# Token blocks 1 to 3 transposed by VectorE in 32 by 32 blocks by way of DRAM, and a first layer norm by pairs of tiles with the constants loaded behind x

## The chip, the core and the metric

The kernel runs on one core of a Trainium2 chip. The time is the device time of one execution in microseconds (us). The core has five engines that run side by side, each in the order of its own instruction queue: TensorE (PE in the profile; PEld is its weight load), VectorE (DVE), ScalarE (ACT), GpSimd (POOL) and SyncE (SP). DMAs are issued from the queues of SP, ACT and POOL and carried out by 16 DMA engines.

## The reference

The input x is 8 sequences of 256 tokens with 512 features, float32. One layer is computed:

```python
xn = _layernorm(x)                       # over the 512 features
s = attention(xn, wq, wk, wv, wo)        # 32 heads of 128, 8 key/value heads, RoPE,
                                         # causal mask, rescaled scores, softmax
g = silu(ffn(xn, router_w, A, B))        # 4 experts of rank 16, the best 2 per token
out = x + s * g
```

## The kernel before

**Tiling.** The 2048 tokens are worked on in four token blocks (`NTB`) of 512 tokens, two sequences each; a block has four tiles of 128 tokens (`NT`). Within a block there are eight steps, one for each key/value head `g`. A step computes, for the next step, a *quad* of projections (`quad`, L486: the queries of four heads, and now and then keys or values) and, for earlier steps, the scores and the softmax (`softmax`), the weighted values (`values`) and a part of the output projection (`out_project`). Projections are multiplied by a scheme of Strassen's kind with seven products (`piece`, L518), each of 8 weight loads and 8 matmuls in the trace. Their names in the trace are pa, pd and pe with k, q or v behind (keys, queries, values); po belongs to the output projection, sc to the scores, av to the weighted values.

**The input of a block.** The projections need the normalised x transposed, features on partitions. It lies in one tile, XB (`acts[tb][0]`), as four quarters; XT (`acts[tb][1]`) holds four sums and differences of the quarters, made by VectorE (`add_up`, L362). There is one buffer for XB and one for XT, so XB of the next block can only be written when the last projection of the block has read it (the hold `x_hold`, room `X=1`).

`norm(tb)` (L309) makes them. For each of four tiles it loads x on SP (`load`, L319), takes mean and variance on VectorE (`statistics`), the root on ScalarE (`root`), the reciprocal (`invert`) and the normalised tile xn (`normalise`) on VectorE. Then TensorE transposes it against an identity matrix into PSUM (`turn`, L349: four transposes of 128x128, called xp in the trace), and ScalarE copies it to XB (`read`, L354). For block 0 the root is taken tile by tile, for the other blocks once for four tiles.

**The start.** Block 0 has nothing to hide behind. SP loads four tiles of x, then the first weights w (`blocks_of`, L408). ScalarE's queue loads three constants at once: the table tab (L1284: cosines, sines, masks), ra (L1285: router and expert weights, rows of 272 B) and bt (L1286). After the key projection the expert scores of the block are computed (`route`, L1137, called lme in the trace: 16 matmuls on XB and ra).

**The softmax's way through DRAM.** `softmax` normalises the probabilities p on VectorE, turns them there in 32 by 32 blocks (`transpose`, L744, tile blocks), writes them to DRAM with four DMAs on SP (`spread`, L755, tile there) and reads them back transposed with one DMA (`gather`, L764, tile pT), which av needs.

**What sets the order.** No engine's order is written out by hand. Each piece of work is a job with an engine, an estimated duration, a lag after its end (for a DMA) and the jobs it comes after (`Plan.add`, L181). TensorE's pieces are laid in a row (`lay`, L191), which gives each a due time; the others' due times follow from it backwards (L196 to L201). `Plan.run` (L195) then plays the whole in time and emits, for each engine, the ready job that is due first and has room in its buffers (`opens`, `closes`). The engines' queues keep this order on the chip. `norm` of the next block is added in step g = 6, and its four transposes are laid among that step's later pieces (L1323 to L1326):

```python
if tb + 1 < NTB and g == KV - 2:
    turns = norm(tb + 1)
    for t in range(NT):
        later[t] = later[t] + [turns[t]]
```

Of the kernel before, what the change touches and what calls it, by code (L numbers as in the profile page):

```python
# [37 lines left out]
F32 = mybir.dt.float32  # L38
# [6 lines left out]
P = 128  # L45
# [211 lines left out]
def layer(ctx: ExitStack, tc: tile.TileContext, x, wquad, woquad, raT, bT, table, out):  # L257
# [12 lines left out]
    ps_sc = pool("ps_sc", 2, space=PSUM)  # L270
    ps_av = pool("ps_av", 2, space=PSUM)
    bounce = pool("bounce", 4, space=DRAM)
    store = pool("store", 1, space=DRAM)

    tab = keep.tile([P, C_END], F32, tag="tab", name="tab")
# [18 lines left out]
    def hold(tag):  # L294
        return Hold(rooms[tag])
# [6 lines left out]

    keys, vals, queries, probs, attn, acc = {}, {}, {}, {}, {}, {}
    begun = []
    gates, sums_of, acts, weights, x_hold = {}, {}, {}, {}, {}

    def norm(tb):  # L309


        n = f"{tb}"
        xs, box = {}, {}
        xh = [hold("x") for _ in range(NB)]
        mh = [hold("m") for _ in range(NT)]
        ph = [hold("mm") for _ in range(NT)]
        x_hold[tb] = hold("X")

        def load(t):  # L319
            if t % 2 == 0:  # L320
                xs["x", t // 2] = x_pool.tile([P, 2, D], F32, tag="x", name=f"x{tb}_{t}")
            xs[t] = xs["x", t // 2][:, t % 2, :]
            nc.sync.dma_start(out=xs[t], in_=x[bass.ds(tb * TB + t * P, P), :])

        def statistics(t):
            if t == 0:
                box["mv"] = one.tile([P, NT, 2], F32, tag="mv", name=f"mv{n}")
                box["r"] = one.tile([P, NT], F32, tag="rstd", name=f"rstd{n}")
            st = two.tile([P, 6], F32, tag="st", name=f"st{tb}_{t}")
            nc.vector.bn_stats(out=st, in_=xs[t])  # L330
            nc.vector.bn_aggr(out=box["mv"][:, t, :], in_=st)

        def variance(ts):
            nc.vector.tensor_scalar_add(box["r"][:, ts], box["mv"][:, ts, 1], EPS)

        def root(ts):
            nc.scalar.sqrt(box["r"][:, ts], box["r"][:, ts])

        def invert(ts):
            nc.vector.reciprocal(box["r"][:, ts], box["r"][:, ts])  # L340

        def normalise(t):
            xn = box[t] = two.tile([P, D], F32, tag="m", name=f"xn{tb}_{t}")
            nc.vector.tensor_scalar(
                out=xn, in0=xs[t], scalar1=box["mv"][:, t, 0:1], scalar2=box["r"][:, t : t + 1],
                op0=ALU.subtract, op1=ALU.mult,
            )

        def turn(t):  # L349
            pt = box["p", t] = ps_mm.tile([P, 2, 2, P], F32, tag="mm", name=f"xp{tb}_{t}")  # L350
            for c in range(DC):
                nc.tensor.transpose(pt[:, c // 2, c % 2, :], box[t][:, bass.ts(c, P)], ident)

        def read(t):  # L354
            if t == 0:
                acts[tb] = (
                    one.tile([P, 2, NB, 2, S], F32, tag="XB", name=f"XB{tb}"),
                    one.tile([P, 4, 2, S], F32, tag="XT", name=f"XT{tb}"),
                )
            nc.scalar.copy(acts[tb][0][:, :, t // 2, :, bass.ts(t % 2, P)], box["p", t])  # L360

        def add_up(i):  # L362
            XB, XT = acts[tb]
            b11, b12, b21, b22 = XB[:, 0, 0], XB[:, 0, 1], XB[:, 1, 0], XB[:, 1, 1]
            t1, t2, t3, t4 = (XT[:, k] for k in range(4))

            a, b = ((b12, b11), (b22, t1), (b22, b12), (b21, t2))[i]
            nc.vector.tensor_sub(XT[:, i], a, b)

        issues = []  # L370
        for t in range(NT):
            issues.append(
                add("sp", 0.3, lambda t=t: load(t), after=issues[-1:],
                    opens=[xh[t // 2]] if t % 2 == 0 else [])
            )
        loads = [
            add("dma", 0.0, lambda: None, after=[issues[t]], lag=8.5 if tb else 5.0 + 1.3 * t)
            for t in range(NT)
        ]
        sts = [add("dve", 0.9, lambda t=t: statistics(t), after=[loads[t]]) for t in range(NT)]  # L380
        begun.extend(issues)
        done = []

        for ts in [slice(0, NT)] if tb else [slice(t, t + 1) for t in range(NT)]:
            v = add("dve", 0.1, lambda ts=ts: variance(ts), after=sts[ts])
            r = add("act", 2.8 if tb else 0.2, lambda ts=ts: root(ts), after=[v])
            done += [add("dve", 0.1, lambda ts=ts: invert(ts), after=[r])] * len(sts[ts])
        reads, pieces = [], []
        for t in range(NT):
            xn = add("dve", 0.4, lambda t=t: normalise(t), after=[done[t]], opens=[mh[t]], closes=[xh[t // 2]])  # L390
            tp = add("pe", 0.5, lambda t=t: turn(t), after=[xn, identity], opens=[ph[t]], closes=[mh[t]])
            opens = [x_hold[tb]] if t == 0 else []
            after = [tp] + reads[:1]
            reads.append(
                add("act", 0.5, lambda t=t: read(t), after=after, opens=opens, closes=[ph[t]],
                    near=(tp, 0.5))
            )
            pieces.append(tp)
        t1 = add("dve", 0.61, lambda: add_up(0), after=reads)
        t2 = add("dve", 0.61, lambda: add_up(1), after=[t1])  # L400
        t3 = add("dve", 0.61, lambda: add_up(2), after=reads)
        t4 = add("dve", 0.61, lambda: add_up(3), after=[t2])
        acts[tb, "B"], acts[tb, "T"] = reads, [t1, t2, t3, t4]
        return pieces

    def blocks_of(tb, room, ring, source, kept, key, form, first):  # L408
# [1 line left out]

        n = f"{room}{tb}_{key}"
        box, there, holds = {}, {}, {}
        order = (A11, A21, A22, A12, S1, S2, S4) if not tb else form.order

        def load(i):
            w = box[i] = ring.tile([P, 2, 2 * P], F32, tag=room, name=f"{n}_{i}")
# [24 lines left out]
        for i in order[:4]:  # L441
            there[i] = add(
                "sp" if first else "pool", 0.4 if first else 0.8, lambda i=i: load(i), after=issue,
                opens=[holds[i]], lag=10.0 if first else 6.0,
            )
        for i, (to, a, b, op) in enumerate(form.steps):
            there[to] = add(
# [38 lines left out]
    def quad(tb, which, out, room, rows, name):  # L486
# [15 lines left out]
        def product(bank, i, half, b, t, first):  # L502
            if first:
                box[bank] = new(bank)
            ps = box[bank]
            xb = acts[tb][0][:, half, b] if t is None else acts[tb][1][:, t]

            for m in range(2):
                for c in range(2):
# [8 lines left out]
        def piece(bank, i, half, b, t, first, after):  # L518
            return add(
                "pe", 1.73, lambda: product(bank, i, half, b, t, first),  # L520
                after=[there[i]] + (XB if t is None else [XT[t]]) + after,
                opens=[{"pa": pa, "pd": pd, "pe": pe}[bank]] if first else [],
                closes=[wh[i], x_hold[tb]],
            )
# [44 lines left out]
    def rope(src, of, dst, opens, after, name):  # L569
# [21 lines left out]
        def turn():  # L591
# [3 lines left out]
        s1 = add("act", 1.0, lambda: swap(1), after=[s0], closes=[of])  # L595
        c = add(
            "dve", 1.14, lambda: nc.vector.tensor_mul(dst(), split(src()), wide(C_COS)),
            after=after + [tables], opens=opens, closes=[of],
        )
        t = add("dve", 1.14, turn, after=[s1])  # L600
        return add(
# [529 lines left out]
    def experts(tb):  # L1131
# [2 lines left out]
        n = f"e{tb}"  # L1134
        box = {}

        def route():  # L1137
            XB = acts[tb][0]
            lm = box["lm"] = ps_av.tile([P, NT, E + E * R], F32, tag="av", name=f"lm{n}")
            for t in range(NT):  # L1140
                for c in range(DC):
                    nc.tensor.matmul(
                        lm[:, t, :],
                        lhsT=XB[:, c // 2, t // 2, c % 2, bass.ts(t % 2, P)],
                        rhs=ra[:, c, :],
                        start=(c == 0),
                        stop=(c == DC - 1),
                    )

        def rank_them():  # L1150
            lm = box["lm"]
# [43 lines left out]
            nc.scalar.copy(box["gmT"], box["gp"])  # L1195

        lh, th = hold("av"), hold("av")
        p1 = add("pe", 3.75, route, after=acts[tb, "B"] + [tables], opens=[lh], closes=[x_hold[tb]])
        r1 = add("dve", 2.0, rank_them, after=[p1], near=(p1, 2.0))
        r2 = add(  # L1200
            "act", 0.3, lambda: nc.scalar.activation(box["gate"], box["gate"], AF.Exp),
            after=[r1], near=(p1, 4.0),
# [35 lines left out]
            return p  # L1238

        gates[tb] = []  # L1240
        return [p1], [p2], [[silu(t)] for t in range(NT)]

# [20 lines left out]
    def lay(pieces):  # L1265
        for piece in pieces:
            plan.lay(piece)
# [12 lines left out]
    def clear():  # L1280
        nc.gpsimd.memset(probs_sb, 0.0)

    def load_tables():
        nc.scalar.dma_start(out=tab, in_=table)  # L1284
        nc.scalar.dma_start(out=ra, in_=raT.rearrange("(c p) m -> p c m", p=P))  # L1285
        nc.scalar.dma_start(out=bt, in_=bT)  # L1286

    identity = add("pool", 1.5, lambda: make_identity(tc.nc, ident), near=None)
    tables = add("act", 2.0, load_tables, lag=4.0)
    cleared = add("pool", 2.0, clear)  # L1290

    LAG_V = 2
# [2 lines left out]
    def part(make, u):  # L1295
        return make(*units[u]) if 0 <= u < len(units) else []

    lay(norm(0))
    lead = []
    for q in quads[0]:  # L1300
        lead += make_quad(*q)
    silus = {}
    route, turn, silus[0] = experts(0)
    lay(lead[:7] + route + lead[7:14] + turn + lead[14:])

    for n in range(len(steps) + 2):
        last = n >= len(steps)
# [7 lines left out]
        if not last:  # L1315
# [5 lines left out]
            if 0 <= at < NT:  # L1321
                fill += silus[tb][at]
            if tb + 1 < NTB and g == KV - 2:  # L1323
                turns = norm(tb + 1)
                for t in range(NT):
                    later[t] = later[t] + [turns[t]]  # L1326
        later = [piece for some in later for piece in some]
        main = []
        for q in quads[n + 1] if not last else []:
# [47 lines left out]
```

## Time and profile before

| What | Value |
|---|---|
| Median of three runs | 1361.68 us |
| The three runs | 1357.97, 1361.68, 1362.44 us |
| The profiled execution | 1358.35 us |
| Its span, first to last instruction | 1356.6 us |
| Granted TensorE clock | 0.998 of full speed |
| VectorE busy / ScalarE busy / GpSimd busy | 1097.6 / 618.5 / 314.1 us |
| DMA | 275.81 MB, mean 203 GB/s |
| DMA there<-blocks, 192 KB each, issue to landing | 256 issues, 3.7 us median |
| DMA pT<-there, 768 KB each, issue to landing | 64 issues, 5.9 us median |
| Transposes xp of x on TensorE | 64, of which 16 at the start |
| Copies XB<-xp on ScalarE | 16, 0.586 us median |
| First matmul / first matmul of a projection (pak) | 8.5 / 14.0 us |

The profile is of one execution. Times in it count from the start of the span. A group of instructions reads "line engine operation out<-in xcount | busy us, mean ns of one | idle time of the engine before them and what ended it". All rows have line 118, because every operation goes through one helper; the tile names tell them apart. A matmul's end is modelled and overlaps the next start, so the cost of one in a stream without gaps is the distance from its start to the next.

### The profile page before, as it was taken

The page shows a single profiled execution, that of the slowest core. Times are in us where ns is not written, and L with a number is a line of the kernel's source. Part 1 is how long each engine was busy: PE and PEld are TensorE (multiplying, and loading weights), DVE is VectorE, ACT ScalarE, POOL GpSimd, SP SyncE. Part 2 cuts the span into 40 slices and gives each one's busy share as a digit, 9 for nine tenths or more (in the row PEclk, how much of TensorE's full clock was granted, in tenths as well). Part 3 has the DMA queues.
Part 4 walks back from the last instruction along what each step waited for, and adds up shares of the span by engine and source line. Part 5 has one row for each costly group of instructions (what it writes and reads, how often), then busy time and mean ns, then how long its engine had stood idle before and what let it go on. Part 6 is the DMA issues. An engine that isn't in the chain of part 4 may idle for free.

```text
span 1356.6 us, 19913 instructions
## 1 busy us (share of the span) xinstructions
PE 1330.6 (98%) x6512; PEld 1170.4 (86%) x6512; DVE 1097.6 (81%) x2827; ACT 618.5 (46%) x1590; POOL 314.1 (23%) x579
## 2 busy tenths in 40 slices
PE   7999999999999999999999999999999999999997
PEld 6888888888888888888888888888888988888986
DVE  5899989898888769689697875959868877676996
ACT  2465454453534435345453444435443455434621
POOL 2323222222222122221222122222122221222020
PEclk9999999999999999999999999999999999999999
DMA  5578766666766666676766666576676676565583
GB/s 172 180 250 256 216 186 223 217 212 207 242 177 212 207 197 185 202 226 181 215 200 217 200 213 202 171 226 206 178 227 193 197 219 202 188 198 186 156 282 106
DMA packets 106150, 275.81 MB, mean 203 GB/s; under 512 B 16000, under 2 KB 52864, under 8 KB 106048
## 3 DMA queue, kind: packets, MB, share of 16 engines
q0 software_dynamic: 45760, 149.98, 35.6%
q1 hardware_dynamic: 59536, 123.76, 29.9%
q8 instruction: 53, 0.87, 0.2%
q10 hardware_dynamic: 752, 0.80, 0.2%
q14 instruction: 49, 0.40, 0.1%
HBM read 194.79 MB, written 79.69 MB: 202 GB/s over the span
## 4 chain that ended last, share of the span: by engine, by line
PE 83%; DVE 9%; DMA 6%; issue 1%; ACT 1%; SPq 0%; DVEq 0%; ACTq 0%
PE po L118 23%; PE paq L118 14%; PE av L118 10%; PE sc L118 8%; PE pdq L118 7%; PE pak L118 4%; DMA pT<-there 4%; PE pav L118 4%; PE peq L118 3%; PE pdk L118 2%; DMA there<-blocks 2%; PE pdv L118 2%; DVE qTq L118 1%; DVE blocks L118 1%; DVE p L118 1%; DVE acc L118 1%
## 5 line engine op out<-in xcount | busy, mean ns | idle before, releaser
L118 ACT ACTIVATE p<-z,least 128x256 f32<-128x256 f32 (+7 forms) x512 | 207.6, 407 | 184.5 <-DVE least L118 137.0
L118 PE MATMUL po<-wo,a 128*128 128x256 f32 x992 | 233.3, 379 | 0.0
L118 PEld LDWEIGHTS po<-wo,a 128*128 128x128 f32 x992 | 186.4, 190 | 22.8
L118 PE MATMUL av<-pT,v 128*128 128x256 f32 x768 | 186.9, 383 | 9.4 <-DMA pT<-there 9.4
L118 DVE CUSTOM_DVE_ANT_0 z<-sc,tab 128x256 f32<-128x256 f32 (+7 forms) x512 | 134.0, 300 | 62.7 <-PE sc L118 59.3
L118 PE MATMUL paq<-XT,w 128*128 128x256 f32 x768 | 182.1, 380 | 0.3 <-ACT u3q L118 0.3
L118 PE MATMUL po<-wo,s 128*128 128x256 f32 x744 | 177.4, 381 | 0.2 <-PE av L118 0.2
L118 PEld LDWEIGHTS av<-pT,v 128*128 128x128 f32 x768 | 145.8, 192 | 30.8 <-issue 5.3
L118 PEld LDWEIGHTS sc<-kk,qTq 128*128 128x128 f32 x1024 | 159.0, 191 | 12.5 <-issue 0.8
L118 PE MATMUL sc<-kk,qTq 128*128 128x256 f32 (+7 forms) x1024 | 167.9, 302 | 0.1
L118 PEld LDWEIGHTS paq<-XT,w 128*128 128x128 f32 x768 | 144.9, 190 | 20.4 <-ACT u2q L118 0.8
L118 DVE TENSOR_TENSOR acc<-acc,po 128x512 f32<-128x512 f32 x189 | 128.2, 679 | 40.5 <-PE po L118 39.1
L118 POOL DMA_DIRECT2D w<-sums x144 | 78.9, 548 | 352.9 <-PE paq L118 158.7
L118 PEld LDWEIGHTS po<-wo,s 128*128 128x128 f32 x744 | 139.6, 190 | 23.7 <-issue 5.5
L118 ACT COPY a<-av 128x512 f32<-128x512 f32 x128 | 74.2, 580 | 179.6 <-PE av L118 179.2
L118 ACT COPY swq<-cq 64x1024 f32<-64x1024 f32 x128 | 133.7, 1045 | 15.0 <-DVE cq L118 10.7
L118 POOL DMA_DIRECT2D w<-in_wquad_dram x148 | 80.9, 548 | 244.9 <-PE paq L118 82.8
L118 DVE STREAM_TRANSPOSE blocks<-p 128x1024 f32<-128x1024 f32 (+1 forms) x128 | 123.6, 968 | 0.2
L118 DVE TENSOR_SCALAR p<-p,total 128x256 f32<-128x256 f32 (+7 forms) x512 | 117.1, 294 | 2.3
L118 DVE TENSOR_TENSOR qTq<-cq,tab 128x1024 f32<-128x1024 f32 x64 | 78.1, 1220 | 30.6 <-ACT cq L118 30.6
L118 ACT ACTIVATION_READ_ACCUMULATOR p<-z,least 128x1 f32 x512 | 95.8, 187 | 0.0
L118 POOL DMA_DIRECT2D wo<-in_woquad_dram x104 | 56.9, 548 | 128.4 <-PE po L118 118.5
(134 smaller groups left out, 1862.3 us busy)
## 6 DMA issues: line engine op xcount, KB each, us to landing
there<-blocks SPq DMA_DIRECT2D x256, 192.0 KB, 3.7
pT<-there SPq DMA_DIRECT2D x64, 768.0 KB, 5.9
w<-in_wquad_dram POOLq DMA_DIRECT2D x148, 256.0 KB, 4.5
w<-sums POOLq DMA_DIRECT2D x144, 256.0 KB, 4.0
wo<-in_woquad_dram POOLq DMA_DIRECT2D x104, 256.0 KB, 5.1
wo<-osums POOLq DMA_DIRECT2D x96, 256.0 KB, 5.0
sums<-w POOLq DMA_DIRECT2D x48, 256.0 KB, 4.2
osums<-wo POOLq DMA_DIRECT2D x32, 256.0 KB, 4.3
```

Source lines behind the costliest of these rows:

```text
L118: ins = what(*args, **kwargs)
```

## The change

It has three parts.

1. *Blocks 1 to 3* are no longer transposed by TensorE. VectorE turns each normalised tile in 32 by 32 blocks into the buffer of its x pair (`turn_blocks`). For each pair of tiles (each half `b`, one sequence) SP writes the blocks to a DRAM tile with four DMAs (`spread`: runs of 1 KB), and reads them back into XB with four DMAs (`gather`: 8 runs of 128 B per partition). The first gather opens the hold on XB; the second comes after the first. PSUM and ScalarE's copies are not used for these blocks. The pair index becomes the outer one in XB, and a product on half `b` waits for that half alone.
2. *Block 0* keeps the TensorE transposes. Its root is taken for two tiles at a time, and the statistics of the second pair come after the first pair is normalised. The first two products are laid ahead of the third and fourth transposes, and the first weights are loaded in another order.
3. *The constants:* tab and bt are loaded on ScalarE's queue after the first copy to XB; ra is laid out on the host in rows of 1088 B and is loaded on SP, after the loads of x. `route` is split into four jobs, one per tile.

The estimated lags of the loads are changed as well. The order of TensorE's queue changes in a few places: at each change of block, four output products and a score group come before the first product on XT; lme is split and, in block 0, half of it comes before the first product on XT. The core of the diff:

```diff
+    def load_tables():
+        nc.scalar.dma_start(out=tab, in_=table)
+        nc.scalar.dma_start(out=bt, in_=bT)
...
-        ph = [hold("mm") for _ in range(NT)]
+        ph = [hold("mm") for _ in range(0 if tb else NT)]
...
+        def turn_blocks(t):
+
+            to = xs["x", t // 2].rearrange("p t d -> p (t d)")
+            nc.vector.transpose(
+                to.rearrange("p (q k t s) -> p t k q s", q=NQ, k=DC, t=2)[:, t % 2],
+                box[t].rearrange("p (k q s) -> p k q s", q=NQ, s=BLK),
+            )
+
+        def spread(b):
+            there = box["there", b] = turned.tile(
+                [NQ, BLK, NQ, 2 * P], F32, tag=f"turned{b}", name=f"turned{tb}_{b}"
             )
+            for a in range(NQ):
+                nc.sync.dma_start(
+                    out=there[:, :, a, :].rearrange("q r e -> r q e"),
+                    in_=xs["x", b][bass.ts(a, BLK)]
+                    .rearrange("r t d -> r (t d)").rearrange("r (q e) -> r q e", q=NQ),
                 )
+
+        def gather(b):
+            if b == 0:
+                new_acts()
+            to = acts[tb][0][:, b].rearrange("p h c (t a s) -> p a (h c t) s", t=2, a=NQ)
+            for a in range(NQ):
+                nc.sync.dma_start(
+                    out=to[:, a],
+                    in_=box["there", b][:, :, a, :].rearrange("q r (k s) -> (q r) k s", s=BLK),
+                )
...
-        sts = [add("dve", 0.9, lambda t=t: statistics(t), after=[loads[t]]) for t in range(NT)]
...
-        for ts in [slice(0, NT)] if tb else [slice(t, t + 1) for t in range(NT)]:
-            v = add("dve", 0.1, lambda ts=ts: variance(ts), after=sts[ts])
+        xn = []
+        for ts in [slice(0, NT)] if tb else [slice(0, 2), slice(2, NT)]:
+            tiles = range(ts.start, ts.stop)
+            sts = [
+                add("dve", 0.9, lambda t=t: statistics(t), after=[loads[t]] + xn[-1:])
+                for t in tiles
+            ]
+            v = add("dve", 0.1, lambda ts=ts: variance(ts), after=sts)
             r = add("act", 2.8 if tb else 0.2, lambda ts=ts: root(ts), after=[v])
...
+        if tb:
+            for b in range(NB):
+                turns = [
+                    add("dve", 0.6, lambda t=t: turn_blocks(t), after=xn[2 * b : 2 * b + 2], closes=[mh[t], xh[b]])
+                    for t in (2 * b, 2 * b + 1)
+                ]
+                out_ = add("sp", 2.4, lambda b=b: spread(b), after=turns, closes=[xh[b]], lag=3.4)
+                reads += [
+                    add("sp", 2.4, lambda b=b: gather(b), after=[out_] + reads[:1],
+                        opens=[] if b else [x_hold[tb]], lag=7.0)
+                ] * 2
+        for t in [] if tb else range(NT):
+            tp = add("pe", 0.5, lambda t=t: turn(t), after=[xn[t], identity], opens=[ph[t]], closes=[mh[t]])
...
+            loaded["ra"] = add(
+                "sp", 0.3, lambda: nc.sync.dma_start(out=ra, in_=raT), after=issues, lag=6.0
+            )
+            loaded["turned"] = pieces[-1]
+            loaded["tab"] = add("act", 1.0, load_tables, after=reads[:1], lag=6.0)
...
-        order = (A11, A21, A22, A12, S1, S2, S4) if not tb else form.order
+        order = (A11, A12, A21, A22, S1, S2, S4) if first else form.order
+        if not tb and not first:
+            order = (A11, A21, A22, A12, S1, S2, S4)
...
-                after=[there[i]] + (XB if t is None else [XT[t]]) + after,
+                after=[there[i]] + (XB[2 * b : 2 * b + 2] if t is None else [XT[t]]) + after,
...
-        p1 = add("pe", 3.75, route, after=acts[tb, "B"] + [tables], opens=[lh], closes=[x_hold[tb]])
+        routes = []
+        for t in range(NT):
+            routes.append(
+                add("pe", 0.94, lambda t=t: route(t),
+                    after=[acts[tb, "B"][t], loaded["ra"], loaded["turned"]] + routes[:1],
+                    opens=[] if t else [lh], closes=[x_hold[tb]])
+            )
...
-    lay(lead[:7] + route + lead[7:14] + turn + lead[14:])
+    lay(tiles[:2] + lead[:1] + tiles[2:] + lead[1:7] + route + lead[7:14] + turn + lead[14:])
...
-                turns = norm(tb + 1)
-                for t in range(NT):
-                    later[t] = later[t] + [turns[t]]
+                norm(tb + 1)
```

## Prediction

> **What bounds the kernel now.** I read the engine totals first, then what TensorE waits for, then the stretches that the change touches.
>
> The first line is from the page (busy us, share), the others from the waits (us in total, times, longest).
>
> ```profile
> PE 1330.6 (98%) x6512; PEld 1170.4 (86%) x6512; DVE 1097.6 (81%) x2827; ACT 618.5 (46%) x1590; POOL 314.1 (23%) x579
> PE av L118 <- DMA pT<-there: 9.4, 6, 2.4
> PE xp L118 <- DVE rstd L118: 8.9, 2, 8.5
> ```
>
> TensorE (PE) is busy for 98% of the span. Of the rest, about 9 us pass before its first matmul, 9.4 us are six waits for transposed probabilities, and the remainder is the tail. So time is won by taking work off TensorE or by starting it earlier, and lost wherever its in-order queue has to wait. The second view is the TensorE timeline at the change from token block 0 to 1 (columns: start, us, engine, line):
>
> ```profile
> 287.58 1.89 PE L118 MATMUL pdq<-XB,w 128*128 128x256 f32 x8
> 289.31 0.75 PE L118 MATMUL sc<-kk,qTq 128*128 128x96 f32 x6
> 289.90 1.97 PE L118 MATMUL po<-wo,s 128*128 128x256 f32 x8
> 291.71 0.60 PE L118 MATMUL xp<-ident,xn 128*128 128x128 f32 x4
> 292.14 1.89 PE L118 MATMUL po<-wo,a 128*128 128x256 f32 x8
> 293.87 0.60 PE L118 MATMUL xp<-ident,xn 128*128 128x128 f32 x4
> 294.31 1.46 PE L118 MATMUL av<-pT,v 128*128 128x256 f32 x6
> 295.61 0.97 PE L118 MATMUL sc<-kk,qTq 128*128 128x256 f32 x4
> 296.42 1.89 PE L118 MATMUL po<-wo,a 128*128 128x256 f32 x8
> 298.14 1.04 PE L118 MATMUL xp<-ident,xn 128*128 128x128 f32 x8
> 299.02 1.46 PE L118 MATMUL av<-pT,v 128*128 128x256 f32 x6
> 300.32 1.57 PE L118 MATMUL sc<-kk,qTq 128*128 128x192 f32 x12
> ```
>
> Here TensorE has no gap. The xp rows are the transposes of the next block. From one start to the next, four of them cost 292.14 - 291.71 = 0.43 us; the eight cost 0.88.
>
> **Part 1, transposes off TensorE (blocks 1 to 3).** Twelve tiles at 0.435 us leave a stream without gaps: **-5.2 us**. The twelve ScalarE copies out of PSUM (0.586 us each) go too, at no gain, since ScalarE is busy 46%.
>
> The row speaks first: a transpose takes 0.11 us of this stream. The Trainium skill ("VectorE: DVE Perf Modes", "Rules for kernel authors" and "The three transpose paths") speaks against the change: for 128x128 it says to use TensorE where PSUM will do, because VectorE turns only 32x32 blocks, and gives 390 ns on TensorE and 311 ns on VectorE for bf16. By its 390 ns the 48 transposes would be worth 18.7 us (an estimate from that page) instead of 5.2; the trace decides.
>
> Added on VectorE: twelve 32x32 block transposes of 128x512. The first line is a group by form (busy us, mean ns), the second a stretch of 5 us with the busy time of PE, PEld, DVE, ACT and POOL, the clock, the DMA share and GB/s.
>
> ```profile
> L118 DVE STREAM_TRANSPOSE blocks<-p 128x512 f32<-128x512 f32 x64 | 44.7, 698 | 0.0
> 275.00:280.00 5.00, 5.00 (x27) 4.51 (x26) 4.90 (x15) 3.62 (x8) 0.55 (x1) 1.00 0.84 269
> ```
>
> They write runs of 32, which no row shows; the bounds are 0.70 (this row) and 1.24 us (the 128x1024 form), and I take 0.70 because the size is the same: 2.8 us per block. VectorE is nearly full there (4.90 of 5 us). But in the changed order the four statistics pairs, which ran from 263.84 to 276.5 (4 x 0.86 = 3.4 us), go ahead of that stretch, to about 245 to 258, where VectorE idles 0.3 to 1.05 us at a time. I cost the sum at nothing; without that cover it is at most 2.8 to 5 us per block for what is queued behind on VectorE, first the scores' statistics, and with them the probabilities.
>
> **Part 2, the way through DRAM.** Per block, VectorE's blocks are written to DRAM by two spreads of four DMAs, and read back by two gathers of four. SP issues all of them in order; four issues of there<-blocks take about 2.2 us. First gather: it waits for the last reader of the old XB, the pdq group that ends by 289.5. It must have landed when the new block's first matmul can run: 301.72 before, less four transposes (1.74), 300.0. Slack, about **10.1 us** after the semaphore. The other two changes of block have the same distance (pdq 620.07, pak 634.21; pdq 952.22, pak 966.36). Queued behind the waiting gather on SP is the probability spread of step 6 (issued at 297.72), so nothing is late there.
>
> Second gather: it stands behind that spread, and its DMAs reuse the completion lanes of the first gather, so it starts near 299, or after the first has landed. XT needs all of XB. In the changed order the first matmul on XT comes after pak, pek, four po groups, two score groups and av, at about 313.2. Two VectorE subtractions and hops take 1.5 us. If a gather takes G, the stall per change of block is the larger of G - 10.1 and 2G - 21.8.
>
> What is G? Each DMA writes 128 partitions x 8 runs of 128 B, so each of 16 engines handles 4 x 64 = 256 small packets per gather. No row has 128 B packets. Nearest are the 272 B rows of ra, on ScalarE's queue (q10) in the first 30 us; the columns are packets, MB, and the share of 16 engines in that time:
>
> ```profile
> q1 hardware_dynamic: 1728, 3.15, 35.9%
> q0 software_dynamic: 400, 1.31, 12.3%
> q10 hardware_dynamic: 752, 0.80, 8.5%
> ```
>
> q10 took 0.085 x 16 x 30 = 40.8 us for 752 packets: 128 of tab (4160 B), 64 of bt (2 KB), 512 of ra and 48 completions. q0's 320 packets of 4 KB took 59 us with their completions, so tab costs 0.15 to 0.18 us each; q1 gives 0.075 to 0.105 for 2 KB. That leaves 11 to 17 us for 560 packets: **20 to 30 ns** each. So G is 256 x 20 to 30 ns plus 2.2 us for issue and landing: 7.3 to 9.9 us. The other end is there<-blocks itself: a burst of four near 963 us took some 113 ns of engine time per 1536 B packet; at that price G is 31. From below, bytes alone, by pT's 768 KB in 5.9 us, give 3.9 + 2.2 = 6.1. I take 8.5 (ra is the nearest row: small runs, DRAM to SBUF). Around the first change other traffic fills 0.66 and then 0.42 of the DMA time (0.2 to 0.4 at the other two), which can add 3 us: stall there about 1.4, none at the others. The spreads also go ahead of a probability gather on SP, issued at 281.67 before and now after about 285; landing takes 5.9, its reader is at 293.4, which leaves 2 us. Together I allow **+1.5 us**.
>
> By itself: the Trainium skill ("DMA: Bandwidth & Descriptors", "Specifications") says that transfers below 512 B lose line rate, against this 128 B gather, and gives some 27 GiB/s per engine; a 128 B packet priced like 512 B would take 18 ns, and G would be 6.7 us (an estimate from that page).
>
> **Part 3, the start.** Before, tab, ra and bt shared the DMA engines with x. From the timeline:
>
> ```profile
> 5.60 0.69 DVE L118 BATCH_NORM_STATS2 st<-x 128x6 f32<-128x512 f32 x1 [5.60 <-DMA x<-in_x_dram]
> 8.75 0.69 DVE L118 BATCH_NORM_STATS2 st<-x 128x6 f32<-128x512 f32 x1 [0.31 <-DMA x<-in_x_dram]
> 19.17 1.89 PE L118 MATMUL pak<-XT,w 128*128 128x256 f32 x8
> ```
>
> Now only x and w are ahead. I take the first tile at 4.4 (bounds: 5.60 as before, and 3.3, the issue plus the 2.6 us that the quickest 256 KB DMA takes). Then two statistics pairs (2 x 0.88), the root (0.65), two normalisations (0.95) and transposes and copies (about 2.3) bring pak to about 10.1; it started at 14.02. pak runs its slow first 3.4 us as before (0.43 per matmul against 0.22 later). In the changed order xp2, xp3 and half of lme (1.76) come before the first matmul on XT, which I work out at 18.35. Before, it was at 19.17 to 19.33 without that half: 1.0 + 1.76 = **-2.7 us** (bounds: 0 and -4.1, the whole move of pak). ra now arrives on SP behind four w tiles; 2.2 MB at the 0.36 MB/us seen there is 9 us, before its use at 16.5.
>
> **Sum.** -5.2 + 1.5 - 2.7 = -6.4 us. Against the profiled execution (span 1356.6, time 1358.35) this gives 1352.0; its time lies 3.3 below the median of the runs, 1361.68. I forecast from the median: **1355.3**.
>
> **Rivals.**
> - *The gathers are late* (slower). If small packets cost more than about 40 ns, G passes 12.2, where 2G - 21.8 = 2.6 eats a third of the 7.9 gained at each of three changes. At 50 ns G is 15, the stall 8.2 x 3 = 24.6, the time 1361.7 - 7.9 + 24.6 = 1378. For it: 0.6 DMA share, the 113 ns of the burst, and VectorE waiting in order behind XT. Against it: q10's 30 ns.
> - *The wait only moves* (same). The spreads, 1 MB per block in a stretch with 0.74 to 0.92 DMA share, delay the probability gather beyond its 2 us, or VectorE's 2.8 us show. At 2 us per change: -7.9 + 6 = -2, 1359.8. For it: six such waits already exist, of up to 2.4 us. Against it: none lies in these stretches.
> - *The start does not move* (the change doesn't do that part): x is bound by latency, not by the tables. -5.2 + 1.5 = -3.7 gives 1358.0, and -5.2 without the stall 1356.5: on the edge.
>
> **How the numbers follow.** 0.3% is 4.1 us, about what a measurement can tell. Forecast 0.55 (own range 1351 to 1357.5), late gathers 0.23, moved wait 0.13, no start 0.09, half of that within 0.3%. So faster 0.59, same 0.18, slower 0.23. The range, 1348 to 1369: below, all of the start's 4.1 and no stall, from the profiled time; above, G = 13.4 (stall 5.0 at each change). Beyond that lies the rest of the first rival, under 0.2.
>
> **What would show it.** No xp after 20 us; pak near 10; XB<-turned landing within 10 us of the pdq group's end; TensorE without a wait on XB or XT at the three changes, and none new on pT. A wait of some us on XB or XT refutes part 2; a first pak after 13 refutes part 3.

## The result and the profile after

| | Before | After |
|---|---|---|
| Median in the same batch | 1361.54 us (1357.97 to 1362.44, 4 runs) | 1350.14 us (1346.91 to 1350.92, 4 runs) |
| Profiled execution: time, span | 1358.35, 1356.6 us | 1350.19, 1348.4 us |

The ratio is **0.993** (95% interval 0.9906 to 0.9953): 9.5 us faster, 6.4 to 12.8. Below, a ratio is turned into microseconds by 1360 us, since the median of the kernel before lay between 1356.5 and 1361.5 us in the batches.

The forecast was 1355.3 us, 6.4 less. The measured time lies in the range given (1348 to 1369), just under the forecast's own narrower one (1351 to 1357.5), and it is faster, as forecast. But the profile shows that two of the three steps did not go as written. The waits of TensorE in the changed kernel (us in total, times, longest):

```profile
PE av L118 <- DMA pT<-there: 8.0, 6, 3.0
PE xp L118 <- DVE xn L118: 7.6, 2, 6.6
PE pak L118 <- DMA w<-in_wquad_dram: 0.8, 1, 0.8
```

No wait on XB or XT: the way through DRAM is quick enough, at the first change by 0.6 us only (XB has landed at 298.26, its first reader starts at 298.89) and by 3.5 and 3.1 at the other two. But pT still makes TensorE wait six times, three of them (312, 645 and 976 us) where it did not before. The second change of block, first on SP, then on TensorE:

```profile
620.54 3.93 SPq L118 DMA_DIRECT2D XB<-turned  x4
628.92 2.25 SPq L118 DMA_DIRECT2D there<-blocks  x4
631.22 3.68 SPq L118 DMA_DIRECT2D XB<-turned  x4
635.07 3.19 SPq L118 DMA_DIRECT2D pT<-there  x1
```

```profile
639.62 3.62 PE L118 MATMUL po<-wo,a 128*128 128x256 f32 x16
645.53 2.54 PE L118 MATMUL av<-pT,v 128*128 128x256 f32 x6 [2.29 <-DMA pT<-there]
647.86 2.65 PE L118 MATMUL pak<-XT,w 128*128 128x256 f32 x8
```

The gather of the probabilities of step 6 stands behind the second gather of XB on SP, and its own issue takes 3.19 us instead of 0.34. av waits 2.29 us for it, and then runs slow, 2.54 us for six matmuls that otherwise take 1.53. At the third change pT's issue takes 3.48 us. At the first, the four DMAs of the gather ahead of it take longer and pT less:

```profile
299.67 5.55 SPq L118 DMA_DIRECT2D XB<-turned  x4
305.39 0.55 SPq L118 DMA_DIRECT2D pT<-there  x1
```

The wait of av is 0.84 us at the first change and 0.20 at the third. There was none at these places before.

The start, and the new transposes on VectorE (a group by form: busy us, mean ns of one):

```profile
3.57 0.69 DVE L118 BATCH_NORM_STATS2 st<-x 128x6 f32<-128x512 f32 x1 [3.57 <-DMA x<-in_x_dram]
...
9.35 3.75 PE L118 MATMUL pak<-XB,w 128*128 128x256 f32 x8 [0.78 <-DMA w<-in_wquad_dram]
...
19.19 1.08 PE L118 MATMUL pdk<-XT,w 128*128 128x256 f32 x4
```

```profile
L118 DVE STREAM_TRANSPOSE x<-xn 128x512 f32<-128x512 f32 x12 | 7.8, 687 | 0.0
```

The waits near 439, 771, 1104 and 1324 us, which cost the kernel before 7.0 us, are gone or under 0.3 us. (Two others, near 115 and 396, are 2.97 and 1.50 us after 1.87 and 0.50.) Nothing in the prediction did that. The SP queue of step 1 shows what is new there; of the kernel before, and then of the changed one:

```profile
1087.52 2.30 SPq L118 DMA_DIRECT2D there<-blocks  x4
1093.13 0.34 SPq L118 DMA_DIRECT2D g<-gates  x1
1095.18 0.34 SPq L118 DMA_DIRECT2D pT<-there  x1
```

```profile
1085.13 2.23 SPq L118 DMA_DIRECT2D there<-blocks  x4
1092.28 0.34 SPq L118 DMA_DIRECT2D pT<-there  x1
1092.66 0.43 SPq L118 DMA_DIRECT2D g<-gates  x1
```

In step 1 of blocks 1 to 3, g (gates, 512 KB, needed later) was ahead of pT (needed next) and is now behind it. The change splits the expert scores (`route`) of each block into four jobs; the planner then takes the softmax of step 1 a little earlier and g falls behind (the split alone does it, e_split below).

### The profile page after: what moved, and what is told of

Same layout as the page of the kernel before. It is cut to its first block, busy times and chain, and to the rows that moved or that the text cites. A ratio compares the mean times of both kernels' runs of the same rounds, so it can differ in the third digit from the quotient of the medians.

```text
span 1348.4 us, 19893 instructions
## 1 busy us (share of the span) xinstructions
PE 1325.3 (98%) x6464; PEld 1165.7 (86%) x6464; DVE 1104.6 (82%) x2835; ACT 611.1 (45%) x1576; POOL 314.3 (23%) x579
## 4 chain that ended last, share of the span: by engine, by line
PE 75%; DVE 14%; DMA 6%; SPq 2%; issue 1%; ACT 1%; DVEq 0%; ACTq 0%
PE po L118 20%; PE paq L118 14%; PE av L118 9%; PE sc L118 7%; PE pdq L118 6%; DMA pT<-there 4%; PE pak L118 4%; PE pav L118 4%; PE peq L118 3%; DVE blocks L118 2%; PE pdk L118 2%; DVE acc L118 2%; SPq L118 2%; DVE qTq L118 2%; DVE p L118 2%; PE pdv L118 2%
## 5 line engine op out<-in xcount | busy, mean ns | idle before, releaser
L118 PEld LDWEIGHTS sc<-kk,qTq 128*128 128x128 f32 x1024 | 159.1, 191 | 12.8 <-DVE p L118 0.8
L118 POOL DMA_DIRECT2D wo<-in_woquad_dram x104 | 56.9, 548 | 130.8 <-PE po L118 120.7
```

The lines of the kernel that those rows point to most:

```text
L118: ins = what(*args, **kwargs)
```

## The experiments

Each ratio is to the kernel before in the same batch (four kernels, four, three and one).

| Run | What it is | Median, us | Ratio (95%) | us |
|---|---|---|---|---|
| e_start | new start, split scores, TensorE transposes | 1349.86 | 0.9932 (0.9911 to 0.9952) | -9.2 |
| e_turn | way through DRAM alone | 1356.75 | 0.9981 (0.9965 to 0.9998) | -2.6 |
| e_early | changed kernel, second gather issued earlier | 1345.94 | 0.9907 (0.9884 to 0.9929) | -12.6 |
| e_wide | changed kernel, small runs in the spreads | 1353.62 | 0.9959 (0.9942 to 0.9977) | -5.6 |
| e_gorder | before, pT ahead of g | 1352.88 | 0.9963 (0.9948 to 0.9978) | -5.0 |
| e_split | before, split scores | 1351.58 | 0.9949 (0.9931 to 0.9967) | -6.9 |
| e_whole | e_start, scores in one job | 1357.19 | 0.9999 (0.9982 to 1.0015) | -0.1 |
| e_after_whole | changed kernel, scores in one job | 1356.28 | 0.998 (0.9965 to 0.9994) | -2.7 |
| e_twice | changed kernel, every XB gather twice | 1411.76 | 1.0397 (1.0357 to 1.0437) | +54 |
| e_half | changed kernel, 64 B packets | 1367.23 | 1.0054 (1.0029 to 1.0078) | +7.3 |

**First question: which part brought it?** In e_start and e_turn, theory A keeps the prediction's sizes (the start is worth up to 3 us, the way through DRAM less than its 5.2); theory B holds in e_start that the start is worth 5 us or more, and in e_turn that the way through DRAM is. The theories of the later runs are named in each expectation.

*e_start*: the whole new start, blocks 1 to 3 transposed by TensorE as before (`if tb:` around the new way becomes `if False:`, and `turn`/`read` run for all tiles).

> The new start alone (constants behind x, pairs of tiles, split expert scores); blocks 1 to 3 are transposed by TensorE as before. Theory A (the start is worth little, since the first wait on a probability gather near 115 us takes most of it back): the first projection matmul starts near 9.4 us instead of 14.0, TensorE is 1.6 us ahead at 60 us, 0.5 us ahead after 115 us, no wait at the three changes of block; 0 to 3 us faster than the kernel before. Theory B (the start is what made the whole kernel faster): 5 us or more faster.

9.2 us faster: A fell. The part without the way through DRAM does as much as the whole change. But the trace does not say that the *start* did it. The table shows the lead of TensorE, the us by which the same groups of matmuls start earlier than in the profiled execution before (median of the groups within 6 us):

| at (us, before) | 100 | 121 | 287 | 430 | 785 | 1115 | 1350 |
|---|---|---|---|---|---|---|---|
| e_start | 1.8 | -0.1 | -0.1 | -0.1 | 2.8 | 5.5 | 8.3 |
| e_whole | 1.8 | -2.1 | -2.1 | -2.2 | -5.4 | -4.3 | -0.9 |
| e_gorder | 0.3 | 0.9 | 0.9 | 1.2 | 2.0 | 4.1 | 6.5 |
| e_after_whole | 1.2 | 2.1 | 2.8 | 3.2 | -0.4 | -0.3 | 3.2 |
| changed kernel | 1.6 | 0.5 | 1.1 | 0.7 | 0.6 | 4.6 | 8.2 |

The lead of the new start is gone at 121 us, behind a wait on pT; e_start gains later, around 439, 771, 1104 and 1324 us. (All five gain some 3 us after 1324, because the execution before waited 2.12 us there and ran slow after it.) Where the start's lead went, each time the kernel before and then e_start: 97 to 105 us (busy time of PE, PEld, DVE, ACT, POOL, clock, DMA share, GB/s), and av:

```profile
97.00:105.00 8.00, 8.00 (x45) 7.25 (x44) 7.96 (x18) 5.34 (x12) 4.00 (x9) 1.00 0.92 289
```

```profile
97.00:105.00 8.00, 8.00 (x44) 7.11 (x43) 7.93 (x25) 6.01 (x18) 4.33 (x8) 1.00 0.96 295
```

```profile
114.99 2.83 PE L118 MATMUL av<-pT,v 128*128 128x256 f32 x12 [1.87 <-DMA pT<-there]
```

```profile
113.48 4.44 PE L118 MATMUL av<-pT,v 128*128 128x256 f32 x12 [2.19 <-DMA pT<-there]
```

The DMA engines are 0.96 busy there (0.92 in the kernel before). e_start issues the spread 1.84 us earlier (97.02 against 98.86), but pT only 0.39 us earlier (104.84 against 105.23). TensorE arrives earlier and waits longer, and the twelve matmuls after the wait take 4.44 us instead of 2.83. Part of that is the single execution: in a second profile of the kernel before the same wait is 2.34 us and the matmuls behind it take 4.21. Over all 14 profiles the loss stands out all the same. The nine with the new start lead by 1.2 to 2.8 us at 111 us (median 1.9) and by -2.1 to 2.1 at 121 (median 0.1); the five with the old start have medians of 0.3 and 0.

*e_turn*: the way through DRAM for blocks 1 to 3 alone; old start, scores in one job.

> The way through DRAM alone (blocks 1 to 3), with the start of the kernel before. Theory A (the 5.2 us of transposes are won, and most is given back to a new wait on the probability gather of step 6, which stands behind the second gather of XB on SP): TensorE waits for pT at the changes of block 1 to 3 us each, with the slower matmuls behind it 0.5 to 4 us each; 0 to 4 us faster than the kernel before. Theory B (the change of block is free, the wait seen there came from the earlier start): no such wait, 5 us or more faster.

2.6 us faster: A held in its time. The new waits at the changes are there, 0.88, 2.29 (at 648.30) and 0.62 us, two of them shorter than A said, and the waits of step 1 too (2.65, 2.15 and 1.58 us).

**Second question: what eats the 5.2 us at the changes of block?**

*e_early*: the second gather is issued right behind the first, ahead of the spread of step 6:

```diff
-                reads += [
-                    add("sp", 2.4, lambda b=b: gather(b), after=[out_] + reads[:1],
-                        opens=[] if b else [x_hold[tb]], lag=7.0)
-                ] * 2
+                sent.append(add("sp", 2.4, lambda b=b: gather(b), after=[out_] + sent,
+                    opens=[] if b else [x_hold[tb]]))
+                reads += [add("dma", 0.0, lambda: None, after=[sent[b]], lag=7.0)] * 2
```

> The changed kernel, but the second gather of XB is issued right behind the first, ahead of the probability spread of step 6, and not after the first has landed. Theory A (the new wait is the second gather's small packets in front of the probability gather): the wait on pT of step 6 goes, its issue takes 0.3 to 0.5 us instead of 3.2 to 3.5; 4 to 6 us faster than the changed kernel, 1344 to 1346. Theory B (the DMA engines are simply full there, wherever the packets stand): the wait stays or moves to the spread or to the first matmul on XB; within 2 us of the changed kernel.

The waits on pT at the changes are gone. At the first change TensorE still stands for 1.06 us ahead of its first matmul on XT ("issue" in the waits), after VectorE had waited 2.06 us for a spread to land. It is the quickest of all by its median, 3.1 us under the changed kernel by the ratios where A said 4 to 6, and the two intervals overlap. Its SP queue at the second change:

```profile
622.03 9.77 SPq L118 DMA_DIRECT2D XB<-turned  x8
631.89 3.06 SPq L118 DMA_DIRECT2D there<-blocks  x4
638.01 0.34 SPq L118 DMA_DIRECT2D pT<-there  x1
```

pT is issued in 0.34 us again: six microseconds lie between it and the last gather of XB, which has landed by then (634.48).

*e_wide*: the spreads write runs of 128 B, and the gathers read rows of 4 KB (the access patterns of both DMAs change with the tile).

```diff
-                [NQ, BLK, NQ, 2 * P], F32, tag=f"turned{b}", name=f"turned{tb}_{b}"
+                [BLK, NQ, NQ * 2 * P], F32, tag=f"turned{b}", name=f"turned{tb}_{b}"
```

> The changed kernel with the small packets moved from the gathers to the spreads: the spread writes runs of 128 B, and the gather reads rows of 4 KB. The bytes are the same, the number of packets is about the same, but they go when nothing waits for XB. Theory A (the number of packets ahead of the probability gather of step 6 makes the wait): a gather lands within 4 us instead of 7 to 8, the wait on pT of step 6 goes; the spread is slower and can delay the probability gather of step 5 by 1 to 3 us; 2 to 6 us faster than the changed kernel. Theory B (bytes and the number of DMAs count, not packets): as the changed kernel within 2 us, with the wait at step 6 unchanged.

5.6 us faster than before, but 3.9 slower than the changed kernel, where A said 2 to 6 faster. The waits of step 6 went, and pT is issued in 0.34 us there. With the same bytes in rows of 4 KB, the four DMAs of a gather are issued in 1.7 to 2.9 us, at the first change:

```profile
293.07 2.60 SPq L118 DMA_DIRECT2D XB<-turned  x4
```

The small writes take the time instead: the eight DMAs of the spreads ahead of the pT of step 5 take 12.9 us to issue at the first change, and

```profile
302.22 2.93 PE L118 MATMUL av<-pT,v 128*128 128x256 f32 x6 [9.04 <-DMA pT<-there]
```

That is the rival "the wait only moves", at 9 us, once.

**Third question: is it the order of g and pT on SP?**

*e_gorder*: g's load of half 1 gets the gather of pT as a predecessor; nothing else in the kernel before is edited. TensorE's, ScalarE's and GpSimd's orders stay; on VectorE some block transposes move up.

```diff
+        if (tb, g, b) in later_g:
+            sent = add("sp", 0.35, gather, after=[out_], opens=[th])
+            sent.then.append(later_g[tb, g, b])
+            later_g[tb, g, b].waits += 1
+            in_ = add("dma", 0.0, lambda: None, after=[sent], lag=7.0)
```

> The kernel before, with one thing changed: in step 1 of blocks 1 to 3 the load of the gates (g of half 1, 512 KB) is issued behind the gather of the probabilities (pT of half 0) on SP, and not ahead of it; two block transposes move up by two places on VectorE with it. TensorE's order is that of before. Theory O (the gain that the sum missed comes from the order of g and pT on SP): the waits of av on pT near 438, 771 and 1104 us go (1.0, 1.4 and 2.4 us with the slower matmuls behind them), so 3 to 5.5 us faster, 1355.5 to 1358 beside 1361. Theory D (splitting the expert scores moves the softmax of step 1 up, and that alone makes pT early): within 1 us of before, the waits stay. Theory S (it is the earlier start that shifts the collisions): within 1 us of before.

5.0 us faster: theory O. Three exchanges on SP, with the block transposes that move along, do half of what the whole change does. The wait near 1104, in the kernel before and then here:

```profile
1104.20 1.53 PE L118 MATMUL av<-pT,v 128*128 128x256 f32 x6 [2.44 <-DMA pT<-there]
```

```profile
1100.06 1.53 PE L118 MATMUL av<-pT,v 128*128 128x256 f32 x6 [0.28 <-DMA pT<-there]
```

From the issue of pT to the start of av it is 9.0 us before and 7.2 here (1095.18, 1092.88); near 439 8.5 and 7.4; near 771 6.6 and 6.5, and there the wait stayed, 1.38 us.

*e_split*: the kernel before with `route(t)` as four jobs, 0.94 us each, one per tile.

> The kernel before, with the expert scores as four jobs of one tile each, and nothing else: start and input transposes are those of before. On SP this puts pT ahead of g in step 1 of blocks 1 to 3, and the planner also takes the softmax of that step a little earlier. Theory O and theory D: the waits near 438, 771 and 1104 us go, 3 to 6 us faster, 1355 to 1358. Theory S: within 1 us of before.

6.9 us faster, and all three waits gone. So the split, which has no term in the prediction's sum, brings the gain alone. D by itself fell with e_gorder, where the order alone brings 5.0 us; whether the earlier softmax adds to it is the 1.9 us between the two runs, which the intervals don't tell apart.

*e_whole*:

```diff
+        routes = [
+            add("pe", 3.75, lambda: [route(t) for t in range(NT)],
+                after=acts[tb, "B"] + [loaded["ra"], loaded["turned"]], opens=[lh], closes=[x_hold[tb]])
+        ] if tb else []
-        for t in range(NT):
+        for t in range(0 if tb else NT):
```

> The new start with constants behind x and pairs of tiles, all inputs transposed by TensorE, but the expert scores of blocks 1 to 3 in one job as before, so that g is ahead of pT on SP again. Against the same kernel with four jobs (1349.9, 9.7 us under before). Theories O and D: the waits near 438, 771 and 1104 us are back, 1355 to 1359, 1 to 4 us faster than before. Theory S: 1349 to 1352, the waits stay away.

The waits are back (1.94, 1.99 and 1.33 us) and so is the time: the new start alone is worth 0.1 us (from 2.4 faster to 2.0 slower).

*e_after_whole*: the same edit in the changed kernel.

> The changed kernel with the expert scores of blocks 1 to 3 in one job as before: the start, VectorE's transposes and the way through DRAM are all there, g is ahead of pT on SP. This is the change as the prediction priced it, without the reordering. Theories O and D: the waits near 438, 771 and 1104 us are back, 3 to 6 us slower than the changed kernel, 1353 to 1356, so that my sum (1355.3) would hold for it. Theory S: 1349 to 1351, as the changed kernel.

2.7 us faster than before, 6.8 slower than the changed kernel, with the waits back (1.66, 1.73 and 2.97 us): O and D. This is the change as the prediction priced it, and it agrees with its parts, 2.6 of e_turn and 0.1 of e_whole.

**Fourth question: how near are the gathers to deciding, and are single waits to be trusted?**

*e_twice*: each XB gather DMA issued twice.

> The changed kernel with every gather of XB issued twice (the same bytes to the same place), so 16 DMAs of 1024 packets of 128 B at a change instead of 8; all else is in the order of the changed kernel. Theory Q (the limit at a change is SP: the probability gather of step 6 stands behind the gathers and their slow issue): by 14 ns for a packet one more half is 4096 x 14 ns / 16 = 3.6 us of all DMA engines, and pT of step 6 lands 3.6 to 8 us later, so its waits (0.8, 2.3 and 0.2 us) grow to 4 to 10 us each, 11 to 24 us slower than the changed kernel, with the wait on pT. Theory X (my rival of the prediction: the gathers decide, through XB and XT): TensorE waits on XB or XT at each change by 2G - 21.8; with G grown from 6.8 to between 10.4 and 13.6 that is nothing to 5.4 us each, and pT shows no more than now.

```profile
PE av L118 <- DMA pT<-there: 34.4, 6, 10.3
PE pak L118 <- DMA XB<-turned: 26.2, 3, 9.7
```

Neither theory's sizes held, and the run did not measure what it was made for. The program lets a second DMA to the same place wait on SP until the first has landed. SP's own waits say so:

```profile
SPq L118 <- DMA XB<-turned: 79.1, 24, 6.5
```

24 waits of 3.3 us in 24 pairs: the gathers ran in series, and a half took 16.0 to 18.5 us to issue. It does show what late gathers cost: 8.0 to 9.7 us on XB and 9.0 to 10.3 on pT at each change. And it shows a second thing: with at most two of these DMAs under way at a time, each is issued in 0.36 to 0.89 us, though its 1024 packets of 128 B are those of the changed kernel. Two in a row:

```profile
656.41 0.98 SPq L118 DMA_DIRECT2D XB<-turned  x2
```

*e_half*: the repair. Each gather DMA is split in two, over different halves of the runs:

```diff
+                for u in (slice(0, BLK // 2), slice(BLK // 2, BLK)):
-                    out=to[:, a],
+                        out=to[:, a, :, u],
```

> The changed kernel with every gather DMA of XB split in two that take one half of each run of 32: the same bytes, but 64 B packets, twice as many (8192 instead of 4096 for a half), in 16 DMAs per change instead of 8. Unlike the run with every gather twice, no DMA writes where another has written, so none waits for the landing of its own pair. Theory P (a small packet costs its 14 ns whatever its size): a half takes 8192 x 14 ns / 16 = 7.2 us of all DMA engines instead of 3.6, G grows from 6.8 to some 10.4, just past the slack of 10.1: 0 to 1 us of wait on XB, and pT of step 6, behind it on SP, lands 3.6 to 7 us later; 10 to 24 us slower than the changed kernel in all. Theory B (the price is by bytes): within 2 us of the changed kernel, XB without a wait.

16.9 us slower than the changed kernel, by the ratios: theory P. The second change:

```profile
638.75 10.89 SPq L118 DMA_DIRECT2D XB<-turned  x8
649.68 0.58 SPq L118 DMA_DIRECT2D pT<-there  x1
```

```profile
655.97 2.93 PE L118 MATMUL av<-pT,v 128*128 128x256 f32 x6 [4.92 <-DMA pT<-there]
```

The bytes are the same, yet eight DMAs of 1024 packets take 8.1 to 10.9 us to issue, where four took 3.6 to 6.2. The run doubles DMAs and packets at once; the packet records of the traces tell them apart: a 64 B packet takes 10.8 ns of a DMA engine here, a 128 B packet 13.6 in the changed kernel. Half the bytes save a fifth, so the price goes mostly by the packet, at a little less than P's 14 ns. XB makes TensorE wait hardly at all, once 3.2 us at the first change (shown as "issue"); pT of step 6 3.2, 4.9 and 4.7 us.

*Second profiles* of both kernels, one execution each (1359.77 and 1346.35 us).

> The kernel before, once more, for a second profile: how far the single waits of av on pT repeat. If they are the kernel's own, the waits near 115, 439, 771, 1104 and 1324 us are there again, within half a microsecond each, and the clock after the ones near 1104 and 1324 is as before. If a wait of this length is a matter of the single execution, they move by a microsecond or more and the sum of 9.4 us is good to some 3 us only.

> The changed kernel, once more, for a second profile. The waits of step 6 near 312, 646 and 976 us (0.8, 2.3, 0.2) should be there again, most near 646, and none on XB or XT, with none or small ones near 438, 771 and 1104. If the lengths move by a microsecond or more, the ledger of single waits holds in sum only.

```profile
774.38 2.22 PE L118 MATMUL av<-pT,v 128*128 128x256 f32 x6 [2.51 <-DMA pT<-there]
```

```profile
643.46 1.56 PE L118 MATMUL av<-pT,v 128*128 128x256 f32 x6 [1.12 <-DMA pT<-there]
```

The places mostly repeat, the lengths don't: near 771 it was 1.41 and is 2.51; near 1324 2.12 and 0.96; at the second change of the changed kernel 2.29 and 1.12. At its first change the 0.84 us at 312 is gone and 0.90 us stands at 292; at the third nothing is left. The sums are nearer: 9.4 and 9.3 us before, 8.0 and 6.4 after. A ledger of single waits is good to a microsecond or so each.

## Why the prediction was right or wrong

**Right in its number by luck, for a partly wrong reason.** The parts it priced bring 2.7 us (0.8 to 4.8), not 6.4 (e_after_whole). What it did not price, the split of the expert scores with the exchange on SP that follows from it, brings the other 6.8. The two misses happen to balance to within 3 us.

- **Part 1, the transposes, -5.2: right.** At each change the changed kernel's lead rises by about 1.75 us, 5.25 in all, until the wait on pT. VectorE's transposes took 0.687 us (0.70 forecast), and TensorE never waits for them.
- **Part 2, the packets: mechanism right, price and place not.** The first gathers had landed 9.8, 7.0 and 7.3 us after their first issue, the second ones 9.8, 9.6 and 9.0 (8.5 forecast), and XB and XT never made TensorE wait, though of the slack of 10.1 us the first change left 0.6. A 128 B packet took 14 ns of a DMA engine, not 20 to 30: in 953 to 962 us of the changed kernel, 39.5% of 16 engines for 9 us are 56.9 us for 4163 packets.

```profile
q1 hardware_dynamic: 4163, 0.54, 39.5%
```

- **Part 2, the queue: the step that failed.** "Queued behind the waiting gather on SP is the probability spread of step 6 ..., so nothing is late there", and "none new on pT". The queue was followed behind the first gather only. Behind the second stands the *gather* of step 6. The issue of an XB DMA was costed like one of there<-blocks, about 0.55 us; it takes 0.9 to 1.5 us, as the mean of four. That is no price of the DMA itself: the first of a change is issued in 0.38 us, in e_twice all in 0.36 to 0.89, and with rows of 4 KB (e_wide) four take 1.7 to 2.9. SP is slow where the small packets of earlier DMAs are still under way; why it is then held up, no run shows. The new waits come to 3.3 us in the changed kernel (0.84, 2.29, 0.20) and 3.8 in e_turn, before the slow matmuls, where 1.5 us were allowed. (e_turn's time alone, 2.6 us of 5.2 with 0.3 to 4.8 about it, would not settle that.)
- **Part 3, the start, -2.7: the step that failed.** The first tile was at 3.57 (4.4 forecast) and pak at 9.35 (10.1); the first XT matmul only at 19.19 (18.35), since pek ran slow too (2.69 us, 1.90 before) and TensorE waited 0.94 us for xn; it led by 1.6 us at 61 us. So 1.6 of the 2.7 arrived, and that lead was carried to the end without a look at the next wait. e_whole measures 0.1 us. (Two slips of the working had no effect: the whole move of pak, 14.02 to 10.1, is 3.9 us and not 4.1; 2.2 MB at 0.36 MB/us is 6.1 us and not 9. ra landed at 11.6, its first reader ran at 17.45.)
- **Missing from the sum.** The order of g on SP was not compared, and the four jobs of the scores enter the sum in block 0 only. The view that would have told is the order of DMAs on SP in steps away from the edit, set beside the 9.4 us of waits on pT that the first view of the prediction shows.
- **The rivals.** *The gathers are late* did not come true, by 0.6 us at the first change; e_twice and e_half show its cost where it does (8.0 to 9.7 us on XB at each change, and 3.2 us at one). *The wait only moves* was half true: it took about half of part 1. *The start does not move* was wrong as written (it moves), but right in its effect.

The Trainium skill ("DMA: Bandwidth & Descriptors", "Specifications") gave an estimate of 6.7 us for a gather. It is nearer than the forecast's own 8.5 to two of the six measured (7.0 and 7.3); the other four (9.0 to 9.8) are nearer to 8.5.

**Open.** What holds SP up behind small packets is not shown. e_start (-9.2) is 2 to 4 us more than e_whole and e_gorder or e_split add up to (-5.1 to -7.0); the intervals are 2 to 3 us wide to each side, and no run settles whether the new start and the order help each other. In the same way the changed kernel (-9.5) is hardly ahead of e_start (-9.2), though the way through DRAM alone is worth 2.6. Whether O or D (pT ahead of g, or the earlier softmax) has more of the 6.8 us is open too.

## What to carry to other kernels

When a plan or scheduler makes the order, compare the order of every DMA queue over the whole kernel, not only at the edit: a job cut into four moved a load in another step, and that was most of the gain. A lead on the busiest engine can end at its next wait; here it ended where the DMA engines were 0.96 busy. For small-packet DMAs, look first at what stands behind them on the issuing queue: several in a row are issued slowly, and here that delayed a stranger's gather before it delayed their own reader. The quickest run, e_early, only put other work between the two.

## What the hardware showed unexpectedly

- **A wait of 2 us can cost 4.** After an idle time TensorE's next matmuls can run slow, with a lower granted clock. Changed kernel at 643 to 649 us, and e_whole at 113 to 119 (the clock is the third number from the end):

```profile
643.00:649.00 6.00, 3.71 (x11) 2.83 (x10) 5.96 (x8) 1.27 (x2) 0.00 (x0) 0.75 0.47 142
```

```profile
113.00:119.00 6.00, 4.96 (x12) 4.00 (x13) 3.46 (x4) 1.82 (x7) 0.54 (x1) 0.53 0.79 193
```

  Over all the profiles here, none of 23 idle times of 0.8 to 1.87 us was followed by slow matmuls; of 28 of 1.91 to 3.22 us 16 were; of nine from 4.7 us on all. It costs some 0.7 to 3 us on top of the wait. The Trainium skill ("TensorE: Matmul & The Clock Gate", "Part 1: The HAM clock gate (the "warmup" mystery)") puts the drop after an idle window of about 3.4 us; here it came after 1.91 us already.
- **A DMA right behind small packets that are still under way is issued late.** Behind the four DMAs of the second XB gather pT's issue took 3.19 and 3.48 us, or the four themselves took longer (5.55, then 0.55 for pT); in a quiet place it takes 0.34. A small-packet DMA with none before it is issued in 0.38 us, nearly as quickly.
- **Half the bytes do not halve a small packet.** 13.6 ns of a DMA engine for 128 B, 10.8 for 64 B (e_half).
